# Moving the layer norms' reciprocal deviations from GpSimd to ScalarE, GpSimd's own work to later places, and the last projections into the next block of rows

## The chip, the cores and the metric

The kernel runs on one core of a Trainium2 chip. The metric is the device time of one execution in microseconds. For the kernel before the change three runs gave 2534.56, 2537.20 and 2538.67, median 2537.2. The profiled execution, from which all the views here come, spans 2561.0 us.

The core has five engines that run their own queues of instructions in order and wait for each other by semaphores: TensorE (PE in the profile; its weight loads are PEld), VectorE (DVE), ScalarE (ACT), GpSimd (POOL), and SyncE (SP), which here only issues transfers.

## The reference, cut to what matters

16 graphs share one adjacency matrix of 1024 nodes; every node has 128 features, and some 8 of 1024 neighbours are set in a row. Four layers follow each other:

```python
# layers 0, 2, 3 (attention with 8 heads of 16)
Q, K, V = h @ Wq, h @ Wk, h @ Wv
scores = where(adj == 0, -inf, einsum(Q, K) / sqrt(16))
x = layer_norm(h + softmax(scores) @ V @ Wo + bo)
x = layer_norm(x + relu(x @ W1 + b1) @ W2 + b2)

# layer 1 (graph attention, one head)
h = x @ W
e = leaky_relu((h @ a_src)[:, :, None] + (h @ a_dst)[:, None, :])
x = layer_norm(softmax(where(adj == 0, -inf, e)) @ h + x)

# layer_norm
(x - mean(x)) * rsqrt(var(x) + 1e-5) * g + b
```

What the change touches is the `rsqrt(var + eps)` of the seven layer norms and the time at which work that surrounds it is issued.

## The kernel before, in words

**Sparse.** Neighbour lists are built first (up to about 190 us). After that each layer is computed from lists: for a block of 128 rows, K and V rows (for the graph layer, h rows) of the neighbours are fetched from a table in DRAM with indirect transfers that GpSimd issues (`gathered`, L856). VectorE multiplies them with the queries (`products`, L868), sums over each head (L891), ScalarE takes the exponential (L895, or L907 in the graph layer), VectorE multiplies values by weights (`weighted`, L919), and TensorE adds up neighbours of the same row by small marking matrices (`summed` and `marked`, L935).

**Units and parts.** The 16 graphs go in two groups of eight, and the 1024 rows in eight tiles, so a layer has 16 units (group, tile), 64 units in all. A unit is cut into parts, each holding two neighbours per row (in the graph layer up to four). An attention unit has five parts as a rule and seven in a group's first tile; its last part is a half-size one (`MIX`), 128x1024 instead of 128x2048. A graph unit has three or four.

**Order.** The order is written out by hand: one loop over parts emits instructions, and each engine runs its share in this order. In iteration i come: products of part i; the summing of part i-2; exponentials of part i; weighting of part i-1; gathers of part i+3. Between these are three slots per iteration (four in the graph layer), `others()`, in which other work goes forward by one step of a Python generator. There are four gather buffers and four product buffers.

**Tails.** When all parts of a unit are summed, `divided` divides by the softmax's denominator and makes two tails, one for each half of the unit's eight graphs. A tail is a generator whose `yield` marks the end of a step. An attention tail's steps are: transpose (L596, evicted at L598) and bias; Wo (L644, L645); the norm; transpose with gain and shift (L600); W1 and Relu (L655, L659); W2 (L664, L668); the norm again; transpose (L600); projection for the next layer in two steps (L538, evicted at L542); writing the table. The second half starts one step later. In the last layer two transposes and a scatter to the output by GpSimd (L625) stand in place of the projection.

**The norm.** `normed` (from L576) has three steps: four Square activations on ScalarE whose accumulators give the variance (L580); one `pow` by -0.5 on a 128x4 tile on GpSimd (L586); four Copy activations with the result as scale (L589). With the pow steps an attention tail has 15 steps, a graph tail 8: these are `STEPS` and `GRAPH_STEPS`.

**Pace.** At each slot `pace` advances, and whenever it passes 1 all tails go forward by one step. It is set so that all steps fall within the next unit's slots: 15 steps in 14 slots for an attention unit of five parts. When the next unit is to be divided (`closing`), `while tails: advance(tails)` first emits all that is left of the old tails; then come the reciprocal (L972), the division (L975), a copy (L984) and the addition of sums into `seen` on GpSimd (L986), all before the next slot.

So on GpSimd's one queue stand the gathers, each of which may wait for a buffer that VectorE has to free, the pows, each of which waits for ScalarE, the additions to `seen` and, in the last layer, the scatters.

Of the kernel before, what the change touches and what calls it, by code (L numbers as in the profile page):

```python
# [11 lines left out]

# [8 lines left out]
P = 128  # L21
# [84 lines left out]

STEPS = 15
GRAPH_STEPS = 8  # L110
EDGES = 4
AHEAD = 4

LIMIT = 1e25


def rows_of(v, n=P):
# [5 lines left out]
def sparse_path(ctx: ExitStack, tc: tile.TileContext, a: dict, out: bass.AP, flag):  # L123
# [27 lines left out]
        q = slice(0, P) if whole else slice(32 * j, 32 * j + 32)  # L151
        return rep[q, j].rearrange("p s n -> p (s n)")

    power = const.tile([P, GH], F32, name="power")
    nc.vector.memset(power, -0.5)

    root = const.tile([P, 1], F32, name="root")
    nc.vector.memset(root, (EPS / D) ** 0.5)
# [416 lines left out]
    def normed(y):  # L575

        z = twos.tile([P, GH, D], F32, tag="o", name="z")
        total = smalls.tile([P, GH], F32, tag="total", name="total")
        for i in range(GH):
            nc.scalar.activation(  # L580
                z[:, i, :], y[:, i, :], AF.Square, scale=D**-0.5, bias=root,
                accum_out=total[:, i : i + 1],
            )
        yield
        rstd = smalls.tile([P, GH], F32, tag="rstd", name="rstd")
        nc.gpsimd.tensor_tensor(rstd, total, power, ALU.pow)  # L586
        yield
        for i in range(GH):
            nc.scalar.activation(z[:, i, :], y[:, i, :], AF.Copy, scale=rstd[:, i : i + 1])  # L589
        return z  # L590

    def turned(z, dst, gain=None, shift=None):

        ps = bank([P, GH, P])
        for i in range(GH):
            nc.tensor.transpose(ps[:, i, :], z[:, i, :], ident)  # L596
        if gain is None:
            nc.scalar.copy(dst, ps)  # L598
        else:
            nc.scalar.activation(dst, ps, AF.Identity, bias=shift, scale=gain)  # L600
# [4 lines left out]
    def finish(l, g, t, h, z, gain, shift):  # L605
        if l + 1 < len(LAYERS):

            wanted[0] = True
            while held[0]:
                advance(slow)  # L610
            wanted[0] = False
            busy[0] += 1
            xn = states.tile([P, GH, P], F32, tag="xT", name="xT")
            turned(z, xn, gain, shift)
            yield
            yield from project(l + 1, g, t, h, xn)
            busy[0] -= 1
            return
        xn = states.tile([P, GH, P], F32, tag="xT", name="xT")
        turned(z, xn, gain, shift)  # L620
        yield
        o = twos.tile([P, GH, D], F32, tag="kv", name="outs")
        turned(xn, o)
        yield
        nc.gpsimd.indirect_dma_start(  # L625
            out=out.rearrange("n (k c) -> (n k) c", k=GR * HF),
            out_offset=bass.IndirectOffsetOnAxis(ap=places[:, g, h, t : t + 1], axis=0),
            in_=o.rearrange("p g d -> p (g d)"), in_offset=None,
        )
# [139 lines left out]
    def is_attention(u):  # L769
        return LAYERS[units[u][0]][1] is ATTN  # L770
# [192 lines left out]
    def divided(u):  # L963

        l, g, t = units[u]
        heads, d = (H, HD) if is_attention(u) else (1, D)
        den = bank([P, G * heads])
        for n, c in enumerate(sum(PIECES[t], [])):
            marked(t, c, den, exs[u][:, n, :])
        both = smalls.tile([P, 2, G * heads], F32, tag="both", name="both")  # L970
        yield
        nc.vector.reciprocal(both[:, 1, :], den)  # L972
        for h in range(HF):
            o = twos.tile([P, GH, D], F32, tag="o", name="o")
            nc.vector.tensor_tensor(  # L975
                o.rearrange("p g (a d) -> p (g a) d", d=d),
                accums[u][:, h, :].rearrange("p (a d) -> p a d", d=d),
                both[:, 1, h * GH * heads : (h + 1) * GH * heads]
                .rearrange("p (a o) -> p a o", o=1)
                .to_broadcast([P, GH * heads, d]),  # L980
                ALU.mult,
            )
            tails.append((attention_tail if heads > 1 else graph_tail)(l, g, t, h, o))
        nc.scalar.copy(both[:, 0, :], den)  # L984
        n = G * heads
        nc.gpsimd.tensor_tensor(seen[:, :, :n], seen[:, :, :n], both, ALU.add)  # L986

# [2 lines left out]
    loads = []  # L990
    slow = []

    def advance(gens):
        for gen in list(gens):
            if next(gen, "end") == "end":
                gens.remove(gen)

    pace = [0.0, 0.0]

# [17 lines left out]
    with tc.manual_schedule():  # L1017
        wide = [gather_buffer() for _ in range(EDGES)]
        setup, entry, weights = graph(wide), at_once(0), load_weights("L0")
        next(setup)  # L1020
        next(weights)
        next(entry)
        more = [weights, load_graph_weights()]
        rest = slots()
        for i, room in enumerate(setup):
            if i == T:
                for gen in more:
                    next(gen)
            if room == "load":
                for _ in loaded(0):  # L1030
                    next(entry, None)
            elif room == "queries":
                for _ in entry:
                    pass
                for _ in queries(0):
                    pass
            elif isinstance(room, str):
                next(rest)
            else:
                for _ in range(room):  # L1040
                    next(entry, None)
        for _ in entry:
            pass
        scratch.close()
        prods = ctx.enter_context(tc.tile_pool(name="prods", bufs=4))
        smalls = ctx.enter_context(tc.tile_pool(name="smalls", bufs=3))
        slow.append(at_leisure(1))
        for i in range(AHEAD - 1):
            gathered(i)
        nc.gpsimd.memset(wide[3], 0.0)  # L1050
        gathered(AHEAD - 1)
        fronts.extend([rest, loaded(1)] + more)
        closing = None
        begun = 0
        for i in range(len(parts) + 2):
            here = i < len(parts)
            u = parts[i][0] if here else len(units)
            if here:
                l = units[u][0]
                if i and parts[i - 1][0] != u:  # L1060
                    begun = i
                    if l + 1 < len(LAYERS) and LAYERS[l + 1][1] is ATTN:
                        if units[u][1:] == (0, 1):
                            more = load_weights(LAYERS[l + 1][0])
                            next(more)
                            next(more)
                        if units[u][1:] == (0, 4):
                            next(more, None)
                if is_attention(u):
                    products(i)  # L1070
            if i > 1:
                summed(i - 2)
                done = parts[i - 2][0]
                if parts[i - 1 : i] == [] or parts[i - 1][0] != done:
                    closing = divided(done)
                    next(closing)
            others()
            if here:
                exponentials(i)
            if here and i == begun + 1:  # L1080
                if is_attention(u):
                    shared(u)
                while loads:
                    advance(loads)
                if u + 1 < len(units):
                    fronts.append(queries(u + 1))
                loads.append(loaded(u + 2))
                if units[u + 2 : u + 3] and units[u + 2][0]:
                    advance(loads)
            others()  # L1090
            if 0 < i <= len(parts):
                weighted(i - 1, 0)
                if not is_attention(parts[i - 1][0]):
                    others()
                    weighted(i - 1, 2)
                gathered(i - 1 + AHEAD)
            if closing is not None and here:
                while tails:
                    advance(tails)
                for _ in closing:  # L1100
                    pass
                closing = None
                passes = 3 if is_attention(u) else 4
                steps = STEPS if is_attention(done) else GRAPH_STEPS
                pace[:] = 0.0, steps / (passes * sum(part[0] == u for part in parts) - 1)
            others()
            if i + 1 >= len(parts) or parts[i + 1][0] != u:

                while fronts:
                    advance(fronts)  # L1110
        while tails:
            advance(tails)
        for _ in closing:
            pass
        while tails:
            advance(tails)
# [434 lines left out]
```

## Time and profile before

| Part of the run | Time of a unit | What is seen |
|---|---|---|
| lists, up to the first division at 189.3 us | | |
| layer 0, from unit 2 on | 40.1 to 59.0 us | group change at 505.8 us the longest |
| layer 1 | 17.8 to 27.0 us | graph layer |
| layers 2 and 3 | 38.0 to 51.7 us | mostly 39 to 42 us |
| after the last division at 2521.2 us | 39.8 us | the last unit's tails alone |

The times of a unit are the distances between the starts of two reciprocals (L972), of which there is one in each unit.

How the views are to be read: the busy shares of the whole page are means over these stages. A view of waits lists who stood still before an instruction and what ended the wait, as total, number and longest. A group of instructions gives count, busy time, mean of one, then the idle time just before them with what ended it. A stretch of the timeline gives start and duration, engine, line, operation, and the idle time before it in brackets.

### The profile page before, as it was taken

To read this page: it belongs to the slowest core of one execution; us is meant where nothing else is said; L and a number is where in the kernel's file an instruction comes from. 1 tells how busy PE (TensorE), PEld (TensorE's weight loads), DVE (VectorE), ACT (ScalarE), POOL (GpSimd) and SP (SyncE) were. 2 spreads that over 40 slices of the span, in tenths; PEclk is the share of its full clock that TensorE was granted. 3 is DMA by queue.
4 is the path that set the end of the run, shared out by engine and by line. 5 is a ranking of instruction groups with operands and counts; after the bars stand their busy time and mean duration, and the time that the engine had idled before them with its cause. 6 is when DMAs were issued, how large, how long until landed. Compare 5 with 4: busy or idle time off the path is not lost. (4 is left out here: it accounts for less than half of the span.)

```text
span 2561.0 us, 36646 instructions
## 1 busy us (share of the span) xinstructions
PE 2102.6 (82%) x13124; PEld 1303.1 (51%) x13124; DVE 1930.3 (75%) x1470; ACT 1474.6 (58%) x4640; POOL 1450.8 (57%) x978
## 2 busy tenths in 40 slices
PE   6558989788887888988788888988888787888786
PEld 5425656445554554554455554555555454445454
DVE  7887787587877466667887879788797877787782
ACT  3216776565665444455476656667666665566555
POOL 3334666366666588784545545455555656665652
PEclk8679999899898999999899999999999898989888
DMA  7646888667678589898777877788777667567660
GB/s 251 232 170 230 293 280 287 210 227 252 231 257 260 175 282 327 281 322 297 276 256 248 298 258 261 255 283 277 264 267 254 222 240 260 203 222 257 222 222 24
DMA packets 168461, 636.05 MB, mean 248 GB/s; under 512 B 38328, under 2 KB 41144, under 8 KB 119774
## 3 DMA queue, kind: packets, MB, share of 16 engines
q0 software_dynamic: 92672, 485.09, 54.2%
q1 hardware_dynamic: 75600, 148.55, 17.4%
q8 instruction: 105, 1.72, 0.3%
q14 instruction: 84, 0.69, 0.1%
HBM read 603.11 MB, written 92.34 MB: 272 GB/s over the span
## 5 line engine op out<-in xcount | busy, mean ns | idle before, releaser
L856 POOL DMA_INDIRECT e<-table,idx x600 | 925.7, 1543 | 455.9 <-DVE pr L919 245.6
L919 DVE TENSOR_TENSOR pr<-e,ex 128x2048 f32<-128x2048 f32 (+1 forms) x336 | 689.5, 2060 | 205.0 <-ACT ex L895 174.2
L868 DVE TENSOR_TENSOR pr<-e,qr 128x2048 f32<-128x2048 f32 x204 | 460.7, 2258 | 177.8 <-PE acc L935 80.7
L586 POOL TENSOR_TENSOR rstd<-total,power 128x4 f32<-128x4 f32 x224 | 333.1, 1490 | 392.6 <-ACT z L580 385.4
L935 PE MATMUL acc<-pr,marks 128*32 128x512 f32 x2656 | 495.1, 618 | 38.2 <-DVE pr L919 38.2
L891 DVE TENSOR_REDUCE sc<-pr 128x128 f32<-128x2048 f32 (+1 forms) x252 | 518.5, 2058 | 8.6
L580 ACT ACTIVATE z<-yps,root 128x128 f32<-128x128 f32 x896 | 318.5, 378 | 98.5 <-PE yps L683 49.8
L596 PE MATMUL ps<-ident,z 128*128 128x128 f32 x896 | 212.7, 338 | 161.8 <-ACT z L589 161.7
L589 ACT ACTIVATE z<-yps,rstd 128x128 f32<-128x128 f32 x896 | 257.3, 381 | 102.4 <-POOL rstd L586 102.3
L596 PEld LDWEIGHTS ps<-ident,z 128*128 128x128 f32 x896 | 136.0, 159 | 345.4 <-ACT z L589 251.8
L659 ACT ACTIVATE f<-ps,b 128x512 f32<-128x512 f32 x192 | 131.9, 690 | 275.8 <-PE ps L655 275.8
L655 PE MATMUL ps<-x,W 128*128 128x512 f32 x384 | 249.1, 783 | 35.9 <-ACT x L600 35.8
L664 PE MATMUL yps<-W,f 128*128 128x128 f32 x1536 | 259.7, 287 | 17.0 <-ACT f L659 15.9
L664 PEld LDWEIGHTS yps<-W,f 128*128 128x128 f32 x1536 | 212.2, 196 | 77.5 <-ACT f L659 58.6
L935 PEld LDWEIGHTS acc<-pr,marks 128*32 128x32 f32 x2656 | 102.0, 112 | 283.8 <-issue 223.9
L538 PE MATMUL ps<-Wkv,xT 128*128 128x256 f32 x768 | 208.7, 416 | 32.7 <-ACT xT L600 24.1
L831 ACT COPY qr<-ps 128x512 f32<-128x512 f32 x384 | 197.0, 600 | 61.3 <-PE ps L828 55.7
L580 ACT ACTIVATION_READ_ACCUMULATOR z<-yps,root 128x1 f32 x896 | 194.1, 217 | 0.0
L542 ACT COPY kv<-ps 128x512 f32<-128x512 f32 x176 | 103.3, 589 | 140.9 <-PE ps L538 117.1
L538 PEld LDWEIGHTS ps<-Wkv,xT 128*128 128x128 f32 x768 | 146.4, 202 | 73.1 <-ACT xT L600 30.0
L644 PE MATMUL yps<-Wo,oT 128*128 128x128 f32 x768 | 160.9, 292 | 6.0 <-ACT oT L598 6.0
L645 PE MATMUL yps<-centre,x 128*128 128x128 f32 x768 | 158.0, 288 | 6.6
(159 smaller groups left out, 2663.6 us busy)
## 6 DMA issues: line engine op xcount, KB each, us to landing
table<-kv SPq DMA_DIRECT2D x88, 512.0 KB
qx<-qr SPq DMA_DIRECT2D x96, 256.0 KB
kept<-xT SPq DMA_DIRECT2D x96, 256.0 KB
x<-kept SPq DMA_DIRECT2D x48, 512.0 KB
e<-table,idx POOLq DMA_INDIRECT x600
table<-kv SPq DMA_DIRECT2D x32, 256.0 KB
edges<-in_adj SPq DMA_DIRECT2D x8, 512.0 KB
spare<-in_x SPq DMA_DIRECT2D x8, 512.0 KB
```

The lines of the kernel that those rows point to most:

```text
L538: nc.tensor.matmul(ps[:, k, :], x[:, i + k, :], w[LAYERS[l][0], "Wkv"], start=True, stop=True,)
L580: nc.scalar.activation(z[:, i, :], y[:, i, :], AF.Square, scale=D**-0.5, bias=root, accum_out=total[:, i : i + 1],)
L586: nc.gpsimd.tensor_tensor(rstd, total, power, ALU.pow)
L589: nc.scalar.activation(z[:, i, :], y[:, i, :], AF.Copy, scale=rstd[:, i : i + 1])
L596: nc.tensor.transpose(ps[:, i, :], z[:, i, :], ident)
L655: nc.tensor.matmul(ps, p["W1"][:, f * P : (f + 1) * P], x1.rearrange("p g n -> p (g n)"), start=True, stop=True,)
L664: nc.tensor.matmul(ps[:, i, :], f1[:, f, i * P : (i + 1) * P], p["W2"][:, f, :], start=(f == 0), stop=False,)
L856: nc.gpsimd.indirect_dma_start(out=es[i][:, k, :], out_offset=None, in_=tables[l, g][:, :], in_offset=bass.IndirectOffsetOnAxis(ap=idx[:, ...
L868: nc.vector.tensor_tensor(prs[i][0][:, :n, :], es[i][:, :n, :ROW], qx[u].rearrange("p (o c) -> p o c", o=1) if (MIX, 0) in piece else of_p ...
L891: nc.vector.tensor_reduce(sc[:, :n, :], prs[i][0][:, :n, :].rearrange("p k (a d) -> p k a d", d=HD), mybir.AxisListType.X, ALU.add,)
L919: nc.vector.tensor_tensor(prs[i][k0 // 2][:, :m, :].rearrange("p k (a d) -> p k a d", d=d), es[i][:, k0 : k0 + m, base : base + ROW].rearr ...
L935: nc.tensor.matmul(outs[32 * j : 32 * j + 32], marks[:, mark, :], rhss, start=(r == 0 and chunk[0] != MIX), stop=(chunk == last),)
```

## The change: what it does and what it is for

1. **Reciprocal deviation on ScalarE.** The pow on GpSimd is replaced by two ScalarE activations, Ln and then Exp with scale -0.5, emitted together with the four Copies. One step of each norm goes away, and the tile of -0.5 with it. A load of the activation tables that hold both functions is put at the start of the program.
2. **Steps.** `STEPS` goes from 15 to 13 and `GRAPH_STEPS` from 8 to 7.
3. **Late projections.** A tail that reaches its projection yields the word "free". When the next unit is to be divided, only tails that aren't free are emitted to this point; the rest of the projection runs in the slots of the next unit, beside the new tails. The pace leaves out `LATE` steps: 1 in layers 0 and 1, 2 in layers 2 and 3.
4. **GpSimd later.** The addition to `seen` comes one iteration later, after that iteration's gathers have been emitted. The scatter of the last layer comes one step later.

It is for taking GpSimd out of the chain of each norm, keeping its gathers free of waits for ScalarE, and not having projections pile up ahead of a division.

```diff
-STEPS = 15
-GRAPH_STEPS = 8
+STEPS = 13
+GRAPH_STEPS = 7
+
+LATE = (1, 1, 2, 2)
...
+BOTH = list(get_activation_tables("gen3")).index("natural_log_exp_and_others")
...
-    power = const.tile([P, GH], F32, name="power")
-    nc.vector.memset(power, -0.5)
+    nc.scalar.add_instruction(
+        mybir.InstLoadActFuncSet(
+            name=nc.get_next_instruction_name(), act_func_set_id=BOTH,
+            engine=mybir.EngineType.Activation,
+        )
+    )
...
         yield
         rstd = smalls.tile([P, GH], F32, tag="rstd", name="rstd")
-        nc.gpsimd.tensor_tensor(rstd, total, power, ALU.pow)
-        yield
+        nc.scalar.activation(rstd, total, AF.Ln)
+        nc.scalar.activation(rstd, rstd, AF.Exp, scale=-0.5)
         for i in range(GH):
             nc.scalar.activation(z[:, i, :], y[:, i, :], AF.Copy, scale=rstd[:, i : i + 1])
...
             turned(z, xn, gain, shift)
-            yield
+            yield "free"
             yield from project(l + 1, g, t, h, xn)
...
         turned(xn, o)
+        yield
         yield
         nc.gpsimd.indirect_dma_start(
...
         nc.scalar.copy(both[:, 0, :], den)
+        yield
         n = G * heads
         nc.gpsimd.tensor_tensor(seen[:, :, :n], seen[:, :, :n], both, ALU.add)
...
-            if next(gen, "end") == "end":
+            got = next(gen, "end")
+            if got == "end":
                 gens.remove(gen)
+            elif got == "free":
+                free.append(gen)
...
                 gathered(i - 1 + AHEAD)
+                for _ in sizes:
+                    pass
             if closing is not None and here:
-                while tails:
+                while any(gen not in free for gen in tails):
                     advance(tails)
-                for _ in closing:
-                    pass
-                closing = None
+                next(closing)
+                sizes, closing = closing, None
                 passes = 3 if is_attention(u) else 4
                 steps = STEPS if is_attention(done) else GRAPH_STEPS
+                steps -= LATE[units[done][0]]
                 pace[:] = 0.0, steps / (passes * sum(part[0] == u for part in parts) - 1)
```

## The prediction

> **What bounds the kernel now.** I read the page's first part, then busy time by stretches, then the waits engine by engine, and last a stretch of the timeline. The first two say that no engine is full:
>
> ```profile
> PE 2102.6 (82%) x13124; PEld 1303.1 (51%) x13124; DVE 1930.3 (75%) x1470; ACT 1474.6 (58%) x4640; POOL 1450.8 (57%) x978
> ```
>
> ```profile
> 1000.00:1100.00 100.00, 90.79 (x568) 49.81 (x568) 62.80 (x80) 45.42 (x162) 79.04 (x61) 0.93 0.85 295
> ...
> 1600.00:1800.00 200.00, 176.36 (x1119) 113.16 (x1118) 163.31 (x92) 134.07 (x402) 103.86 (x72) 0.94 0.80 274
> ...
> 2200.00:2400.00 200.00, 160.90 (x991) 96.40 (x989) 158.25 (x89) 119.44 (x378) 123.18 (x80) 0.91 0.66 234
> ```
>
> The columns are PE, PEld, DVE, ACT and POOL busy, granted clock, DMA share, GB/s. In the graph layer (first row) TensorE, GpSimd and the DMA engines are high and VectorE is not; in the attention layers (the other two) TensorE stands at 80 to 88% and VectorE at 79 to 82%. Two nearly full engines that both still idle mean that they wait for each other. 48 of 64 units are attention units, so VectorE's waits come next, with the shape of the worst:
>
> ```profile
> DVE pr L919 <- ACT ex L895: 174.2, 58, 10.9
> DVE pr L868 <- PE acc L935: 92.1, 26, 9.6
> DVE sc L900 <- DMA e<-table,idx: 78.2, 38, 4.0
> DVE pr L868 <- DMA e<-table,idx: 70.6, 33, 7.9
> DVE both L972 <- PE ps L935: 47.8, 24, 9.0
> ...
> DVE both L972 <- PE ps L538: 11.1, 3, 4.6
> ```
>
> ```profile
> L919 DVE TENSOR_TENSOR pr<-e,ex 128x1024 f32<-128x1024 f32 x72 | 88.1, 1224 | 158.3 <-ACT ex L895 152.0 <-PE ps L596 6.3
> ```
>
> 152.0 of the 174.2 us stand before the half-size weighting, the last part of each of the 48 attention units: 3.2 us a unit. The timeline shows why:
>
> ```profile
> 1508.23 3.78 PE L655 MATMUL ps<-x,W 128*128 128x512 f32 x4 [0.87 <-ACT x L600]
> ...
> 1517.67 1.88 PE L655 MATMUL ps<-x,W 128*128 128x512 f32 x4
> ...
> 1518.73 0.69 ACT L659 ACTIVATE f<-ps,b 128x512 f32<-128x512 f32 x1 [5.05 <-PE ps L655]
> ...
> 1520.17 0.25 ACT L895 ACTIVATE ex<-sc 128x64 f32<-128x64 f32 x1
> ...
> 1520.45 1.23 DVE L919 TENSOR_TENSOR pr<-e,ex 128x1024 f32<-128x1024 f32 x1 [6.13 <-ACT ex L895]
> ```
>
> The exponential stands on ScalarE behind the second half's two Relus; these wait 5.05 us for TensorE's W1, and VectorE waits 6.13 us with them. TensorE is late because of the norm before. The chain of the norm, in the waits of the other engines:
>
> ```profile
> POOL rstd L586 <- ACT z L580: 385.4, 110, 12.7
> ...
> POOL e L856 <- DVE pr L919: 245.6, 62, 21.8
> ...
> PE ps L596 <- ACT z L589: 161.7, 79, 7.7
> ...
> ACT z L589 <- POOL rstd L586: 102.3, 61, 7.6
> ...
> POOL seen L986 <- ACT both L984: 88.9, 31, 10.5
> ```
>
> A pow queues behind a gather that waits for VectorE (245.6 us), ScalarE's Copies wait for the pow (102.3), TensorE's transposes for the Copies (161.7); and gathers queue behind pows and `seen` that wait for ScalarE (385.4 and 88.9). The first W1 group above also ran at half clock, 3.78 us against 1.88, after such a wait: the granted clock was 0.50 from 1507 to 1513 us.
>
> **What the Trainium skill says.** "ScalarE: Activation LUTs", Table sets: Ln and Exp share a set, so no table switch comes with each norm; a load costs about 1283 ns. The trace before has one load, 1.3 us, and the changed program's order of instructions also has just one. The same page, What ACT_TABLE_LOAD costs: an activation with immediates has a fixed 186 ns, of which some 93 overlap back to back; the trace agrees for small ones (185 ns for 128x2, 225 ns for an exponential of 128x8). "TensorE: Matmul & The Clock Gate", Part 1: about 3.4 us with little TensorE work halve its clock, about 3.4 us of work restore it; the trace shows the halving, as above. "GPSIMD Engine Reference", 2.1: each instruction passes two software dispatches and a join of eight cores; the pow of four elements per partition took 1.0 us in its shortest records and 1490 ns in the mean.
>
> **The change part by part.**
>
> *Pow to ScalarE.* GpSimd loses 224 x 1.490 = 333 us busy and 392.6 us of waits ahead of it. ScalarE gains 448 small activations at 0.20 to 0.23 us (the two rows above), about 100 us busy. The changed program makes Ln, Exp and the first Copy each wait on ScalarE's own last result. No trace row shows such a wait; bounds are the lost overlap (0.09 us) and a whole fixed part (0.19), so 0.3 to 0.6 us a norm. I take 0.45: a norm costs ScalarE 0.9 us, 200 us in all, against the 102.3 us of waits that end. Queued behind them are the exponentials; ScalarE stays under 70%, so I cost this at nothing on the path, with up to 60 us for the bad end. The chain from last Square to first Copy was 0.15 + 1.04 + 0.2 us with GpSimd free and up to 7.6 us more with it busy; it becomes 0.9.
>
> *Fewer steps per slot.* 15 steps in 14 slots become 12 (layer 0) or 11 (layers 2 and 3). The order changes with it: the half-size exponential now stands ahead of the second half's Relus, behind only the transposes' eviction, in all attention layers. In the stretch above this eviction ended at 1513.7 us, before the weighting was due at 1514.3, so the 6.13 us wait would be gone. Of 152.0 us I take two thirds, 100 us, as TensorE, 80 to 88% busy, will hand a part back as a wait for product buffers (the 92.1 us row): minus 100, plus 30.
>
> *Late projections and the division.* L972 waits 79 us in all (47.8 + 20.4 + 11.1 over L935, L558, L538), where projections and transposes piled up ahead of it. With tails free at the division nothing is emitted there in layers 0 to 2; the last layer has no projection and still drains. I take 25 us. The work itself stays; it moves beside the next unit's queries and first transposes.
>
> *Gathers earlier.* With no pow and `seen` ahead, gathers wait only for buffers. L868 and L900 wait 70.6 + 78.2 us for data. In the graph layer the DMA engines were at 0.85 and GpSimd at 79%: earlier issue helps by little. I take 20 of 149 us. The scatter, one step later, is hidden by gathers already issued.
>
> *The end.* The last unit's 39.8 us has two exposed norms per half: 4 x 0.5, so 2 us; beside it the DVE memset and table load at the start, nothing (the load moved, the list building hides it).
>
> *Clock.* Half-clock time is (1 - 0.911) x 2 = 18% of the span, some of it idle. If a quarter of the TensorE waits of 161.7 us no longer trip it, I estimate 10 us, half of a few dozen spells of a few us.
>
> Sum: -100 + 30 - 25 - 20 - 2 - 10 = -127 us at full value; VectorE's waits overlap in cause (TensorE is late once, three rows show it), so I take about four fifths: -100 us, **2437 us**. Check on TensorE: its records leave 458 us idle, 161.7 for the norm; losing 100 us there asks for two thirds of it to go.
>
> **The rivals.** *All of it goes*: TensorE, no longer stalled or slowed, keeps up, and VectorE runs near 92% in attention units: its work per unit, from 198 full (2.29 x 3) and 54 half parts (1.22 x 3) over 48 units plus 1.9 us for the division, is 34.4 us, so 37.5 us a unit against 41.5, and 48 x 4.0 = 190 less: **2350 us**. For it: both engines have room; against it: one product wait on TensorE (92.1) isn't touched. *TensorE is the bound*: weights wait less for the exponential but products wait for sums instead, and only the end, some gathers and half the division's waits are gained: 2537 - 2 - 15 - 12 = **2508 us**. For it: 88% in 1600 to 1800; against it: the half-clock spells and 161.7 us of pure waiting. *ScalarE becomes the wait*: self-waits at their upper end on the way to every exponential (0.6 us + 0.45 busy, four norms x 48 units = 200 us, a quarter exposed), and late projections delay the next unit's queries and first exponentials by 0.5 us a unit (24 us), with the gain of the exponential's place lost: 2537 + 50 + 24 - 40 = **2571 us**. For it: ScalarE's queue is strict, and exponentials sit in it between tail steps; against it: it idles over 40% of the span, and the changed order puts exponentials ahead of waits rather than behind.
>
> **How the numbers follow.** Forecast 0.57, all of it 0.15, TensorE the bound 0.18, ScalarE the wait 0.10. The range runs from 2365 (forecast with 70 us more: ex waits wholly gone, clock restored) to 2515 (past the TensorE case), leaving out the ScalarE case and half of the all case. Faster 0.88 (first three, less a small part of the third), same 0.03, slower 0.09.
>
> **What would show it.** Right: no POOL rstd rows; the half-size weighting's wait on ex falls from 152 to some 50 us; PE's wait on z from 161.7 to about 60; clock above 0.92; attention units at 39 to 40 us; ScalarE busy near 1575 us. Wrong: L868's wait on acc above 150 us (TensorE bound), or full-size weighting waiting for ex by more than its 22.2 us (ScalarE), or the division's wait unchanged. Most likely to fail is the share handed back by TensorE.

## The result, and the profile after

The changed kernel took 2427.65 us (2417.41 to 2429.80, four runs) beside 2537.93 us for the kernel before: ratio 0.9554, 95% interval 0.9521 to 0.9588. (The two medians alone give 0.9566.) The forecast was 2437.

The first part of its page, to be read against the one of before:

```profile
PE 2051.9 (85%) x13124; PEld 1287.2 (53%) x13124; DVE 1934.6 (80%) x1469; ACT 1548.5 (64%) x5088; POOL 1025.8 (42%) x754
```

VectorE's work is what it was (1934.6 against 1930.3 us), the span is 145.4 us shorter, 35 us more than the medians say, because the profiled execution of before took 24.8 us more than its kernel's median and that of the changed kernel 10.2 us less. GpSimd lost 425 us busy, more than its 333 us of pows. ScalarE gained 74 us. The waits of VectorE, in the same view as before:

```profile
DVE pr L878 <- DMA e<-table,idx: 102.3, 40, 10.3
DVE pr L878 <- PE acc L945: 83.5, 17, 7.8
DVE sc L910 <- DMA e<-table,idx: 80.5, 31, 6.5
DVE pr L929 <- ACT ex L905: 57.5, 21, 5.1
DVE both L982 <- PE ps L945: 31.0, 14, 10.0
```

```profile
L929 DVE TENSOR_TENSOR pr<-e,ex 128x1024 f32<-128x1024 f32 x72 | 87.8, 1220 | 34.6 <-ACT ex L905 32.9 <-ACT ex L917 0.9 <-PE acc L945 0.8
```

The wait for exponentials fell from 174.2 to 57.5 us, that of the half-size weighting from 152.0 to 32.9, the division's from 79.3 (three rows) to 31.0. The waits for gathered data (the two rows with `e<-table,idx`) rose, from 148.8 to 182.8. From the other engines' waits:

```profile
POOL e L866 <- DVE pr L929: 931.3, 194, 24.4
...
PE ps L605 <- DMA rows<-in_x,places: 65.6, 18, 11.5
...
PE ps L605 <- ACT z L598: 16.5, 16, 2.1
```

TensorE waits for z 16.5 us instead of 161.7. GpSimd stands ready 931.3 us for buffers: a gather is now issued when its buffer comes free. Two TensorE waits have grown: that for layer 0's input rows (33.1 before), and that of the queries' second step for `q` from ScalarE (39.2 us, 12.1 before).

Where the 145 us lie, from the starts of the reciprocals (one a unit), with the experiments' profiles beside them:

| Kernel | layer 0, divisions 2 to 14 | layer 1, 17 to 32 | layers 2 and 3, 33 to 64 |
|---|---|---|---|
| before | 524.6 us | 309.7 | 1275.2 |
| changed | 534.0 | 281.0 | 1169.5 |
| acts_old_steps | 524.6 | 284.5 | 1236.3 |
| norm_only | 526.5 | 287.6 | 1231.5 |
| norm_exp_first | 523.1 | 289.6 | 1247.2 |
| slow_pace_drain | 540.1 | 277.1 | 1175.5 |
| rows_3 | 505.2 | 280.5 | 1172.9 |
| before_rows_3 | 501.9 | 300.7 | 1263.0 |

Layers 2 and 3 give 106 us, layer 1 gives 29, divisions 14 to 17 give 21, the tails at the end 2 (39.8 to 37.8); layer 0 up to division 14 loses 9, and the list building ahead of the first division 3. In layers 2 and 3 a unit went from 41.1 to 37.7 us in the mean. Each row is one execution: before_rows_3 differs from the kernel before in layer 0 alone, and is still 9 and 12 us shorter in the other two columns, so differences of this size between rows say nothing. There are two questions: which part of the change brings the 106, and why layer 0 up to division 14 has none of it.

### The profile page after: what moved, and what is told of

Its sections match the earlier page's. It is cut to its first block, busy times and chain, and to the rows that moved or that the text cites. A ratio compares the mean times of both kernels' runs of the same rounds, so it can differ in the third digit from the quotient of the medians.

```text
span 2415.6 us, 36632 instructions
## 1 busy us (share of the span) xinstructions
PE 2051.9 (85%) x13124; PEld 1287.2 (53%) x13124; DVE 1934.6 (80%) x1469; ACT 1548.5 (64%) x5088; POOL 1025.8 (42%) x754
## 5 line engine op out<-in xcount | busy, mean ns | idle before, releaser
L866 POOL DMA_INDIRECT e<-table,idx x600 | 842.6, 1404 | 1186.8 <-DVE pr L929 931.3
L929 DVE TENSOR_TENSOR pr<-e,ex 128x2048 f32<-128x2048 f32 (+1 forms) x336 | 696.7, 2082 | 70.2 <-ACT ex L905 57.5
L878 DVE TENSOR_TENSOR pr<-e,qr 128x2048 f32<-128x2048 f32 x204 | 460.1, 2256 | 206.0 <-DMA e<-table,idx 102.3
L598 ACT ACTIVATE z<-yps,rstd 128x128 f32<-128x128 f32 x896 | 256.3, 369 | 7.3
L674 PE MATMUL yps<-W,f 128*128 128x128 f32 x1536 | 252.5, 282 | 6.4 <-ACT f L669 1.1
L547 PE MATMUL ps<-Wkv,xT 128*128 128x256 f32 x768 | 221.9, 430 | 18.4 <-ACT xT L607 11.5
L665 PE MATMUL ps<-x,W 128*128 128x512 f32 x384 | 206.5, 665 | 30.3 <-ACT x L609 30.3
L838 PE MATMUL ps<-q,rep 32*128 32x512 f32 x768 | 175.6, 688 | 39.8 <-ACT q L833 39.2
L589 ACT ACTIVATION_READ_ACCUMULATOR z<-yps,root 128x1 f32 x896 | 202.2, 226 | 0.0
L605 PEld LDWEIGHTS ps<-ident,z 128*128 128x128 f32 x896 | 115.8, 144 | 140.9 <-ACT z L598 66.9
L605 PE MATMUL ps<-ident,z 128*128 128x128 f32 x896 | 173.6, 297 | 16.8 <-ACT z L598 16.5
L905 ACT ACTIVATE ex<-sc 128x128 f32<-128x128 f32 (+1 forms) x252 | 78.5, 311 | 150.8 <-DVE sc L901 149.4
```

Source lines behind the costliest of these rows:

```text
L547: nc.tensor.matmul(ps[:, k, :], x[:, i + k, :], w[LAYERS[l][0], "Wkv"], start=True, stop=True,)
L589: nc.scalar.activation(z[:, i, :], y[:, i, :], AF.Square, scale=D**-0.5, bias=root, accum_out=total[:, i : i + 1],)
L665: nc.tensor.matmul(ps, p["W1"][:, f * P : (f + 1) * P], x1.rearrange("p g n -> p (g n)"), start=True, stop=True,)
L674: nc.tensor.matmul(ps[:, i, :], f1[:, f, i * P : (i + 1) * P], p["W2"][:, f, :], start=(f == 0), stop=False,)
L866: nc.gpsimd.indirect_dma_start(out=es[i][:, k, :], out_offset=None, in_=tables[l, g][:, :], in_offset=bass.IndirectOffsetOnAxis(ap=idx[:, ...
L878: nc.vector.tensor_tensor(prs[i][0][:, :n, :], es[i][:, :n, :ROW], qx[u].rearrange("p (o c) -> p o c", o=1) if (MIX, 0) in piece else of_p ...
```

## The experiments

They ran on several chips, on which the kernel before took 2537.9 to 2560.2 us; so ratios to the kernel before on the same chip are compared, not times. The changed kernel itself was not run again on these chips, and whether it varies with the chip as the kernel before does isn't known; differences of half a per cent between ratios from different chips aren't told apart.

**1. ScalarE alone: acts_old_steps.** The kernel before with only the engine changed.

```diff
-        nc.gpsimd.tensor_tensor(rstd, total, power, ALU.pow)
+        nc.scalar.activation(rstd, total, AF.Ln)
+        nc.scalar.activation(rstd, rstd, AF.Exp, scale=-0.5)
         yield
         for i in range(GH):
```

> The kernel before with the pow replaced by Ln and Exp on ScalarE and nothing else: the step of the pow and all places stay (15 and 8 steps, no late projections, GpSimd's additions and scatters where they were). In the attention layers the half-size exponential still stands behind both of the second half's Relus. Place theory (most of the gain is where the half-size exponential and the last projections stand): 2505 to 2540 us, the half-size weighting still waits over 110 of its 152 us for the exponential. Engine theory (most of the gain is GpSimd leaving the norm's chain, so that TensorE no longer waits for z): 2450 to 2485 us, TensorE's wait on z falls from 161.7 to under 60 and the half-size weighting's wait to under 80.

Measured 2488.81 us, ratio 0.9761 (0.9716 to 0.9805): between the two theories. Its longest wait on VectorE, and TensorE's for z:

```profile
DVE pr L927 <- ACT ex L903: 170.0, 55, 6.6
```

```profile
PE ps L604 <- ACT z L597: 94.4, 50, 2.3
```

The engine brings about half of the gain, and most of layer 1's (309.7 to 284.5; the changed kernel has 281.0). But the wait for exponentials is as long as before (170.0), and TensorE still waits 94.4 us for z: of the 161.7 us of before, more than half remain without GpSimd in the chain.

**2. One step less in each norm: norm_only.** As 1, and without the `yield` after Exp, so 13 and 7 steps.

> The kernel before with the change's first two parts: Ln and Exp on ScalarE and one step less in each norm (13 and 7 steps), but no late projections and GpSimd's additions and scatters at their old places. The half-size exponential still stands behind the second half's Relus, as 13 steps in 14 slots put it. Place theory: 2500 to 2535 us. Engine theory: 2440 to 2470 us, most of the way to the changed kernel's 2428.

Measured 2499.11 us, ratio 0.9800 (0.9758 to 0.9842). Merging the steps adds nothing to experiment 1 that can be measured. Fewer steps, all still paced out in 14 slots, are no gain. One row of TensorE's waits makes this a test of the norm's chain too:

```profile
PE ps L603 <- ACT z L596: 0.4, 1, 0.4
```

The wait for z is gone altogether, from 94.4 us in acts_old_steps, and the granted clock is 0.940, above the changed kernel's 0.930. The time is no shorter, and VectorE still waits 136.1 us for exponentials. TensorE waits elsewhere instead: 74.6 us for x before W1 (37.0 in acts_old_steps) and 40.7 for `q` (12.8). Even z and x together fell, from 131.4 to 75.0 us.

**3. The changed kernel with GpSimd's pow: pow_new_order.**

```diff
-        nc.scalar.activation(rstd, total, AF.Ln)
-        nc.scalar.activation(rstd, rstd, AF.Exp, scale=-0.5)
+        nc.gpsimd.tensor_tensor(rstd, total, power, ALU.pow)
         for i in range(GH):
```

> The changed kernel with the pow back on GpSimd, emitted in the same step as the Copies, so that the order of all other work is that of the changed kernel: half-size exponential ahead of the second half's Relus, late projections, late additions. Place theory: 2440 to 2470 us. Engine theory: 2500 to 2540 us, TensorE waits for z over 120 us again and GpSimd's pows wait for ScalarE over 300 us.

Measured 2697.35 us, ratio 1.0568 (1.0530 to 1.0607): 5.7% slower than before, outside what either theory gave. ScalarE's and TensorE's waits say why:

```profile
ACT z L600 <- POOL rstd L598: 474.1, 204, 9.8
```

```profile
PE ps L607 <- ACT z L600: 212.6, 122, 7.9
```

With pow and Copies in one step nothing lies between them in ScalarE's queue. ScalarE stands for 204 of 224 pows, 2.3 us each, with exponentials and evictions behind. In the kernel before the step between pow and Copies hid most of this (102.3 us). So the merged step is possible because of Ln and Exp, not a gain beside them.

**4. GpSimd's additions and scatters at their old places: seen_early.**

```diff
-        yield
         yield
         nc.gpsimd.indirect_dma_start(
...
-                next(closing)
-                sizes, closing = closing, None
+                for _ in closing:
+                    pass
+                closing = None
```

> The changed kernel with GpSimd's additions to seen and its output scatters back at their old places, ahead of gathers. Both theories: GpSimd waits some 60 to 90 us for ScalarE there again, but gathers wait 931 us for product buffers anyway, so little reaches VectorE: 2425 to 2440 us.

Measured 2446.11 us, ratio 0.9585 (0.9550 to 0.9620), against 0.9554 (0.9521 to 0.9588). The intervals overlap; the part is worth some 0.3% or nothing. GpSimd waited 51.1 us for ScalarE there and had 910.8 us of waits for buffers to hide it in.

**5. The half-size exponential's place, from below: norm_exp_first.** norm_only with one exponential per attention unit emitted a slot earlier.

```diff
+            first = here and (MIX, 0) in sum(parts[i][1], []) and is_attention(u)
+            if first:
+                exponentials(i)
             others()
-            if here:
+            if here and not first:
                 exponentials(i)
```

> The kernel norm_only (Ln and Exp on ScalarE, 13 and 7 steps, projections drained before the division as in the kernel before) with one swap: in the iteration of an attention unit's half-size part its exponential is emitted one slot earlier, so that it stands ahead of the second half's Relus as in the changed kernel. Nothing else of the late projections is in it. If the place of this exponential is what the late projections bring: ratio 0.955 to 0.965 to the kernel before, and the half-size weighting's wait under 40 us. If what they bring is the free division and the work spread over the next unit: 0.975 to 0.982, with the wait taken up by the division (79.7 us in norm_only) and by products waiting for sums.

Measured 2511.87 us, ratio 0.9798 (0.9756 to 0.9840), the same as norm_only's 0.9800. The wait at that place is gone, from 101.4 us in norm_only to 4.7:

```profile
L926 DVE TENSOR_TENSOR pr<-e,ex 128x1024 f32<-128x1024 f32 x72 | 87.6, 1217 | 11.6 <-ACT ex L914 6.8 <-ACT ex L902 4.7
...
L979 DVE RECIPROCAL both<-ps 128x64 f32<-128x64 f32 x48 | 26.7, 556 | 98.2 <-PE ps L942 76.0 <-PE ps L545 14.5 <-PE ps L565 7.6
```

```profile
DVE pr L875 <- PE acc L942: 110.7, 20, 8.2
```

It has moved to the full-size weightings' wait for exponentials (77.6 us, 34.7 in norm_only), to products that wait for sums (110.7, 70.3) and to the division (98.2, 85.0). The place of the exponential was where TensorE's lateness showed, not its cause.

**6. The same from above: exp_behind.** The changed kernel with this exponential a slot later, behind the second half's Relus, where the kernel before has it.

```diff
+            last = here and (MIX, 0) in sum(parts[i][1], []) and is_attention(u)
-            if here:
+            if here and not last:
                 exponentials(i)
...
             others()
+            if last:
+                exponentials(i)
             if 0 < i <= len(parts):
                 weighted(i - 1, 0)
```

> The changed kernel with the half-size exponential emitted one slot later, behind the second half's Relus where the kernel before had it; all else as changed. If the exponential's place is only where TensorE's lateness shows: ratio 0.953 to 0.963, with a wait of the half-size weighting of 50 to 100 us that replaces other waits. If the place costs by itself once TensorE keeps up: 0.97 to 0.985, with 120 us or more of wait there added to what the changed kernel waits.

Measured 2436.30 us, ratio 0.9589 (0.9546 to 0.9632). The wait is back and the time isn't:

```profile
L929 DVE TENSOR_TENSOR pr<-e,ex 128x1024 f32<-128x1024 f32 x72 | 88.1, 1224 | 130.1 <-ACT ex L905 126.7 <-PE acc L945 2.2 <-ACT ex L917 0.7
```

126.7 us instead of 32.9, and a ratio that is 0.35% of the time of before above the changed kernel's, with intervals that overlap; the wait of products for sums fell from 83.5 to 37.7 us in exchange.

**7. The pace without the overlap: slow_pace_drain.** The changed kernel with the old drain ahead of the division: the projections don't run in the next block, but the pace stays at 11 or 12 steps in 14 slots.

```diff
-                while any(gen not in free for gen in tails):
+                while tails:
                     advance(tails)
```

> The changed kernel with one line back: before a division all that is left of the old tails is emitted (the changed pace stays, 11 or 12 steps in 14 slots, and so does the place of the half-size exponential). Two or three steps of each tail, the projections, then stand in one lump ahead of the division. If the lump ahead of the division is what the late projections take away: ratio 0.975 to 0.99 to the kernel before, the division's wait above 110 us. If the slower pace is the gain in itself: 0.953 to 0.962.

Measured 2431.66 us, ratio 0.9553 (0.9504 to 0.9603): the changed kernel's. The overlap with the next block brings nothing that can be measured. What is left of the change beside norm_only is the slower pace, with the exponential's place that follows from it, and GpSimd's later places; the last two were taken back one at a time in the changed kernel, for 0.35% and 0.3% (experiments 6 and 4), of the 2.5% between norm_only and this kernel. The slower pace alone, on norm_only, was not run. The waits of VectorE over 1240 to 2340 us (within layers 2 and 3), first norm_only, then slow_pace_drain:

```profile
DVE pr L926 <- ACT ex L902: 46.2, 27, 4.3
DVE pr L875 <- DMA e<-table,idx: 37.0, 22, 4.1
DVE both L979 <- PE ps L942: 29.6, 16, 3.6
DVE pr L875 <- PE acc L942: 29.4, 9, 3.4
DVE both L979 <- PE ps L545: 11.3, 5, 3.5
```

```profile
DVE pr L878 <- DMA e<-table,idx: 78.9, 33, 5.2
DVE pr L878 <- PE ps L605: 33.2, 13, 4.4
...
DVE pr L878 <- PE ps L665: 4.2, 5, 1.7
```

And the busy times of both kernels over that stretch, in the same order (columns PE, PEld, DVE, ACT, POOL, clock, DMA share, GB/s):

```profile
1240.00:2340.00 1100.00, 944.78 (x6037) 576.98 (x6035) 926.91 (x524) 752.37 (x2405) 470.86 (x308) 0.97 0.76 265
```

```profile
1240.00:2340.00 1100.00, 989.60 (x6314) 616.66 (x6312) 967.30 (x545) 787.17 (x2515) 454.85 (x322) 0.95 0.77 273
```

VectorE's waits for TensorE and ScalarE, 117 us over four rows with 13 paced steps, are 37 us over two rows (L605 and L665) with the slower pace. What remains is the wait for gathered data, 78.9 us. More work is done in the same stretch at a slightly lower clock (0.95 against 0.97), so the clock is not the gain here.

**8. ScalarE's room: double_acts.** The changed kernel with each Ln and Exp done twice, the first pair into a tile that nobody reads.

```diff
+        spare = smalls.tile([P, GH], F32, tag="spare", name="spare")
+        nc.scalar.activation(spare, total, AF.Ln)
+        nc.scalar.activation(spare, spare, AF.Exp, scale=-0.5)
         nc.scalar.activation(rstd, total, AF.Ln)
```

> The changed kernel with the two small activations of each norm done twice, the first pair into a tile that nobody reads: 448 more activations, some 95 us more busy on ScalarE. If ScalarE has room, as the prediction held, the time stays within 10 us of the changed kernel's: 2425 to 2440 us. If the norm's chain through ScalarE has become the wait, a quarter to a half shows: 2455 to 2480 us. All of it would be 2525 us.

Measured 2455.73 us, ratio 0.9585 (0.9556 to 0.9614) on a chip where the kernel before took 2560.2; 0.3% above the changed kernel's ratio, with intervals that overlap. ScalarE's busy time rose to 1609.5 us. By the ratios, 448 more activations on ScalarE cost some 8 us (0.9585 less 0.9554, of 2538), which the intervals don't tell from nothing. By the times they cost 28 us, and 2455.73 is the lower edge of what the second theory gave; that was written in times, for a chip on which the kernel before takes longer. So ScalarE's room is likely but not settled.

**9. Layer 0 and its input rows: rows_later, rows_3, before_rows_3.** In the changed kernel TensorE waits for input rows that GpSimd fetches; this is one such wait in layer 0, on GpSimd and then on TensorE:

```profile
663.82 2.86 POOL L794 DMA_INDIRECT rows<-in_x,places  x1 [0.16 <-issue]
```

```profile
670.72 1.11 PE L605 MATMUL ps<-ident,rows 128*128 128x128 f32 x4 [5.49 <-DMA rows<-in_x,places]
671.62 3.62 PE L665 MATMUL ps<-x,W 128*128 128x512 f32 x4
```

The transposes stand two slots after the fetch in the hand-written order. TensorE reaches them just as GpSimd issues the fetch, stands for 5.49 us, and does the next W1 in 3.62 us at a granted clock of 0.50, where 1.88 us was seen at full clock. The edit gives the rows one slot more (rows_3) or two (rows_later):

```diff
                 yield "idle"
                 yield "idle"
+                yield "idle"
                 turned(rows, xs[units[u]][:, h])
```

> The changed kernel with the transposes of layer 0's input rows (the rows are fetched by GpSimd's indirect transfer) emitted two slots later, four after the fetch where it was two. TensorE waited 65.6 us for these rows, about 5 us in each unit of layer 0, and products waited for sums behind them. If this is why layer 0 gained nothing (units of 42 to 45 us against 36 to 38 in layers 2 and 3): 2365 to 2400 us, layer 0 units at 38 to 40 us. If layer 0 is held by something else (its additional projections, ScalarE): 2420 to 2432 us, although TensorE's wait for rows goes.

> As rows_later, but with the transposes one slot later (three after the fetch). If the wait for rows is what holds layer 0, half of its effect or more: 2380 to 2410 us. If not: 2420 to 2432 us.

> The kernel before with layer 0's input rows transposed three slots after the fetch instead of two. TensorE waited 33 us for rows there. If the wait for rows is one that the change made bite: ratio 0.995 to 1.003. If the kernel before paid for it too: 0.985 to 0.99.

rows_later: 2415.04 us, ratio 0.9443 (0.9417 to 0.9469). rows_3: 2397.06 us, ratio 0.9361 (0.9336 to 0.9385). before_rows_3: 2532.53 us, ratio 0.9952 (0.9934 to 0.9970). So one slot is worth 1.9% of the time of before in the changed kernel by the ratios (1.2%, 31 us, by the times), and 0.5% in the kernel before. TensorE's wait for rows over 560 to 760 us in rows_3, where the changed kernel waited 24.5 us in that stretch:

```profile
PE ps L605 <- DMA rows<-in_x,places: 1.7, 3, 0.7
```

This wait is a real cost, and a larger one in the changed kernel. But it isn't why layer 0 gains nothing: with the rows moved in both kernels, divisions 2 to 14 take 501.9 us in before_rows_3 and 505.2 in rows_3, and the change still brings nothing there. VectorE's longest waits over these divisions, first before_rows_3 (243 to 745 us), then rows_3 (248 to 754 us):

```profile
DVE pr L920 <- ACT ex L896: 44.8, 18, 5.5
DVE pr L869 <- PE acc L936: 22.5, 8, 4.1
```

```profile
DVE pr L879 <- PE acc L946: 60.9, 10, 7.6
DVE pr L930 <- ACT ex L906: 12.7, 6, 6.0
```

In layer 0 the change turns waits for exponentials into waits of products for TensorE's sums. In layers 2 and 3 (divisions 33 to 64) both fell: from before to the changed kernel, waits for exponentials from 98.1 to 1.9 us and for sums from 47.4 to 10.6. One difference is that TensorE has more to do in layer 0, 36.2 us of work a unit in rows_3 against 34.0 in layers 2 and 3, while VectorE has 33.4 and 33.1; that this is the reason wasn't tried.

rows_later does worse than rows_3, whose wait for rows was small already. Its units 2 and 3 of layer 0 took 56.6 and 53.1 us (50.3 and 42.7 in rows_3), and 33 us of new waits of products are put down to a remote release; its longer row of steps is likely to be forced out at the next unit's start, but this wasn't tried.

**10. More of it: rows_3_late2.** rows_3 with `LATE = (2, 1, 2, 2)`.

> rows_3 (input rows transposed three slots after their fetch) with layer 0 at the pace of layers 2 and 3, two steps late instead of one. If layer 0's remaining distance (38 to 42 us a unit against 36 to 38) comes from its pace: ratio 0.928 to 0.934. If from its additional projections and fetches: 0.934 to 0.940, as rows_3.

Measured 2393.09 us, ratio 0.9409 (0.9368 to 0.9450), against rows_3's 0.9361 (0.9336 to 0.9385). The intervals overlap; no further gain is shown. Both rows_3 and rows_3_late2 beat both kernels.

## Why the prediction was right, and where its reasons weren't

**The time and the bound.** TensorE and VectorE holding each other up was right: with the same work on both, VectorE's waits for the other two fell, and the span with them. The sum of 100 us was within 10 of the 110 measured. Its terms were not, and that they add up to so near a number is in part luck. They were also spread over all 48 attention units, some 2 us each; measured are 3.4 us a unit in layers 2 and 3, none in layer 0 up to division 14, and 29 us in layer 1, for which the sum had nothing but a share of the 20 us of gathers.

**TensorE's wait for the norm, not the measure.** "TensorE is late because of the norm before", and the check that two thirds of the 161.7 us have to go, made this wait the measure of the gain. It isn't: norm_only takes it to 0.4 us and is no faster than acts_old_steps with 94.4 (0.9800 and 0.9761), as other waits took its place.

**Pow to ScalarE, wrongly sized.** The engine was costed at nothing on the path and its gain spread over gathers, clock and end (20 + 10 + 2 us). Experiment 1 shows 0.0239 x 2550 = 61 us from it alone. So a large part of what the forecast booked under the steps and the late projections belonged here. The cost was oversized too: 0.9 us a norm were taken, 0.45 for waiting on its own results. The trace of the changed kernel has

```profile
L598 ACT ACTIVATE z<-yps,rstd 128x128 f32<-128x128 f32 x896 | 256.3, 369 | 7.3
...
L595 ACT ACTIVATE rstd<-total 128x4 f32<-128x4 f32 x224 | 49.5, 221 | 1.7
L596 ACT ACTIVATE rstd<-rstd 128x4 f32<-128x4 f32 x224 | 46.1, 206 | 7.1
```

that is 0.43 us of work and 16.1 us of idle time over all 224 norms, 0.07 each. This is under the lower of the two bounds (0.3), which came from the Trainium skill's "ScalarE: Activation LUTs", What ACT_TABLE_LOAD costs, where activations back to back overlap by 93 ns: the lost overlap was added as idle time to durations of 221 and 206 ns that are measured without any overlap.

**Fewer steps per slot, the step that failed.** "Of 152.0 us I take two thirds, 100 us": the wait did fall to 32.9 us, as forecast, but it is not what was gained. Moving the exponential alone took the same wait away and no time (experiment 5); moving it back restored the wait for some 0.35% of the time (6). What did count in this part is the slower pace of the tails itself, 11 or 12 steps in 14 slots against 13 (experiments 2 and 7: 0.980 and 0.955). And "plus 30" for a share that TensorE hands back came in layer 0 alone: over divisions 2 to 14 products wait 67.9 us for sums instead of 42.9, but in the whole 83.5 instead of 92.1.

**Late projections, right in size for the wait, wrong in cause.** The division's wait fell by 48 us, where 25 were taken. But running projections in the next block isn't what did it: slow_pace_drain puts them in one lump ahead of the division and has the same time (30.9 us of wait at the division). What the late projections bring is that `LATE` steps are taken off the pace.

**Gathers, wrong in sign.** 20 us less were taken; VectorE waits 34 us more for gathered data. The rise lies in layers 2 and 3 (40.9 to 82.9 us), where hardly any other wait is left; in layer 1 the wait fell (76.3 to 65.8). GpSimd is ready earlier, but buffers come free by VectorE (931.3 us of waits there) and units are shorter: the DMA engines moved 288 GB/s from and to the memory over the span, 272 before. In layer 1 they were busy 0.95 of the time, 0.86 before.

**The end and the clock.** 2 us taken, 2.0 found, which is luck: the same stretch takes 37.7 to 43.6 us over the experiments. The clock is 0.930 instead of 0.911 in the profiled executions; what it brought isn't shown by any run, and norm_only is slower at 0.940.

**The rivals.** The forecast lay between two rivals that each described a stage. "All of it goes" gave 37.5 us a unit, and layers 2 and 3 have 37.7. "TensorE is the bound", where products wait for sums in place of exponentials, describes layer 0 up to division 14. There a wait for input rows comes on top, which the prediction left out: the waits of before had it at 33.1 us, and the half clock after a stall, which the Trainium skill's "TensorE: Matmul & The Clock Gate", Part 1, describes, was seen by the prediction at another place alone. Against "ScalarE becomes the wait" stands double_acts, by its ratio; its sign, full-size weightings that wait for exponentials by more than 22.2 us, came by a hair (24.6). pow_new_order is close to what that rival described, with GpSimd in ScalarE's way.

**What stays open.** Why layer 0 up to division 14 gains nothing, whether the slower pace would bring its share without Ln and Exp (the pow in its own step with fewer paced steps was not run), and why a slower pace is faster. Two things go with the pace: heavy steps of both halves (W1, W2) no longer fall into one part's time, and each step has more slots between it and the next, so that its result is ready when TensorE comes to it. TensorE's wait for the evicted x before W1 fell in 1240 to 2340 us from 49.0 us in norm_only to 27.7 in slow_pace_drain, which fits the second, and VectorE's waits for sums fit both. No run tells them apart.

## What to carry to other kernels

In a schedule written by hand, the longest wait of the fullest engine may only be where another engine's lateness comes out: before counting it as gain, ask what ends it next, and test it by moving that one instruction. Steps that are paced out should leave slack against the slots they are given; 13 steps in 14 slots cost some 2.5% here against 11 or 12, whether the rest was overlapped or not. And an instruction that takes a small result through a busy third engine costs by that engine's queue, not by its own length: 1.5 us of pow in the mean became 0.43 us of two activations, and one step of distance less was affordable only then (1.0568 without, 0.9554 with). A wait for a result is not yet a price either: TensorE's wait for the norm went from 94.4 to 0.4 us between experiments 1 and 2, and no time was gained.

## What the runs showed of the hardware that wasn't expected

- A chain of two dependent 128x4 activations, and a Copy that takes their result as scale, ran on ScalarE with 0.07 us of idle time a chain: 221 and 206 ns, and the next began some 0.03 us after the result before it. What such a chain loses is overlap: the norms' Copies of 369 ns each take up 286 ns apiece (256.3 us over 896).
- 600 gathers of the same shapes took 1404 ns each on GpSimd instead of 1543 in the changed kernel, and 1610 in pow_new_order, where the pows are back between them; full-size weightings on VectorE took 2317 ns instead of 2288.
- One stall of 5.49 us on TensorE was followed by W1 matmuls at a granted clock of 0.50 that took 3.62 instead of 1.88 us: the stall cost at least another 1.7 us after its end.
- A shorter wait was followed by half clock too: in the kernel before, the granted clock was 1.00 up to 1506 us and 0.50 from 1507, after one wait of TensorE of 1.93 us; the prediction went by some 3.4 us.
